# The last image's output stage two blocks at a time, its synthesis row by row behind it, in the buffers and banks of the scans

## The chip, the cores and the metric

The kernel runs on one core of a Trainium2 chip. A core has five engines that run their own instruction streams: TensorE (PE, matmuls into PSUM banks), VectorE (DVE), ScalarE (ACT), GpSimd (POOL) and SyncE (SP, used here to issue DMAs). [...] An engine takes its instructions in order, so a DMA issue that has to wait holds up every DMA issue behind it on the same engine. The metric is the device time of one launch in microseconds; lower is better.

## What is computed

The input is x, 8 images of 96 channels with 128 x 128 pixels, all float32. Two layers follow each other. The first is a row by row convolutional LSTM with a residual. The second normalises, splits each image by a wavelet transform into a low band and three high bands of 64 x 64, weights the high bands by a small attention, runs the low band through a selective scan in four directions, and puts the bands together again. Cut to what the change touches, the end of the second layer for one image is:

```
y = out_y[:, 0] + inv_y[:, 0] + wh_y + invwh_y          # sum over the four scan directions
y = layernorm(y, out_norm_w, out_norm_b) * silu(z)
x_ll = y @ out_proj_w.T                                 # "output": 192 -> 96 channels, 64 x 64
x_rec_in = concatenate([x_ll, x_high * attn])           # 4 bands for each channel
x = x + conv_transpose(x_rec_in, rec_w, stride 2)       # "synthesis": 96 channels, 128 x 128
```

## The kernel before

The kernel works through the images one after another. The scans of an image are laid out by hand as a list of slots (the loop over `s` near the end of `forward_kernel`); in each slot the engines do one scan step, and what room is left is filled with jobs of other stages. A job is a Python generator (class `Job`). Each `yield` names an engine, a cost that the planner assumes, a number of slots to wait, and the resources it takes and gives (`free`, line 481: counters of banks and buffers). `add` puts a job on the list, `write` emits as many pieces as fit and whose earlier jobs (`after`) are done, and `pin` fixes the order in which the pieces were emitted as the order of each engine. While image b is scanned, the output and synthesis of image b-1 and the wavelet analysis of image b+1 run as such jobs.

The last image has no scans of another image beside it. When its scans are over, the last lines (1209 to 1212) call `output(B - 1, ...)` and `drain(synthesis(B - 1, ...))`. `drain` sets no limits of room: it emits round after round, in the order of the job list, until all is done. There the order of the work follows from three things only: the `after` lists, the counters in `free`, and the order in which jobs were added.

`output(b, ...)` has 8 jobs, `block(j)` for 512 pixels (8 rows of the low band) each. A job loads the row-order and the column-order sums (y_d), the scan input u and the gate z from DRAM for channels 0 to 127 (first half) and 128 to 191 (second half), lines 843 to 846; adds them on POOL (849) and DVE (851); centres them with two matmuls for each half (`pf`, 859), squares on ACT (862), multiplies by the gate on DVE (864); sums the squares by matmul (`pv`, 868), takes the inverse root on ACT (871, 872); projects to 96 channels (`po`, 876, and `pq`, 883), combines on DVE (879, 886); and stores to ll_d (888). It holds six of the twelve "short" buffers. The tiles `t` and `u` serve both halves, so the second half's loads wait for the first half's adds. Each job has the job before it in `after`.

`synthesis(b, ...)` has 24 jobs, `block(g, j)`: 16 output channels (g, 6 groups) by a quarter of the image (j, 4 rows of blocks). A job loads the high bands (hi_d, 795) and the low band (ll_d, 797) into `ph`, at the upper and lower edge also a row of zeros (`zrow`, 787 and 789), and the pixels to be added to into `raw` (800). Six matmuls follow (`pd`, 811; each appears as two records in the profile), two adds on DVE (817) and four stores (820). `weights(g)` loads a group's weights (774) and scales them by the attention on ACT (777). The buffers `ph`, `raw` and `wg` have two copies each; block j of all groups depends on `after`, which for every image holds all 8 output jobs.

The scans use buffers of their own: `bt` and `ct` (five copies each, 128 x 1024), `xb` (six copies, 128 x 1024), and PSUM tiles `da` (two copies, two banks each) in the pool `psh`. The other stages' matmuls share three banks (tag "mm", counted by "bank").

Of the kernel before, what the change touches and what calls it, by code (L numbers as in the profile page):

```python
# [7 lines left out]
F32 = mybir.dt.float32  # L8
# [6 lines left out]
B, C, H, W = 8, 96, 128, 128  # L15
H2, W2 = H // 2, W // 2
L = H2 * W2
# [7 lines left out]
CH = 512  # L25
NCHK = L // CH
GN = 2
NSHORT = 12
# [28 lines left out]
def forward_kernel(ctx: ExitStack, tc: tile.TileContext, i, out):  # L57
# [29 lines left out]
    with ExitStack() as s:  # L87
# [15 lines left out]
        def place(lanes, chunk, src):  # L103
            for m in range(3):
                nc.sync.dma_start(wq[lanes, chunk, m, 0:96], src[:, m, :])
                nc.sync.dma_start(wq[lanes, chunk, m, 96:128], src[:, 3, 32 * m:32 * m + 32])
# [23 lines left out]
        for k in range(NBLK):  # L130
            xb = blk.tile([128, B, RB * W], F32, name="xb")
# [22 lines left out]
        ps = s.enter_context(tc.tile_pool(name="l0ps", bufs=2, space=PSUM))  # L154
        for k in range(NBLK):
            rows = slice(k * RB, (k + 1) * RB)
            xb = blk.tile([128, B, RB * W], F32, name="xb")
# [43 lines left out]
            for r in range(RB):  # L201
                at = [((r + 2) % 4, k + (r + 2) // 4)]
# [28 lines left out]
    with ExitStack() as s:  # L231
# [105 lines left out]
        io = s.enter_context(tc.tile_pool(name="bio", bufs=2))  # L337
        bcp = s.enter_context(tc.tile_pool(name="bbc", bufs=6))
        sp = s.enter_context(tc.tile_pool(name="bs", bufs=2))
        psh = s.enter_context(tc.tile_pool(name="bpsh", bufs=2, space=PSUM))  # L340
        psy = s.enter_context(tc.tile_pool(name="bpsy", bufs=1, space=PSUM))
        ps = s.enter_context(tc.tile_pool(name="bps", bufs=3, space=PSUM))
# [32 lines left out]
        for k in range(4):  # L375
            r, p, h0 = dtrow[k], k // 2, k % 2
# [76 lines left out]
        def pin():  # L453
            traced = tc.nc.cur_bb.bb.instructions
            for ins in traced[seen[0]:]:
                prev = pinned.get(ins.engine)
                if prev is not None:
                    tc.add_manual_dep(ins, prev.name, mybir.DependencyInfo(
                        mybir.DependencyClass.NoSync, mybir.DependencyReason.DATA), reason="order of the slots")
                pinned[ins.engine] = ins  # L460
            seen[0] = len(traced)
# [16 lines left out]
                    for r in self.give:  # L478
                        free[r] += 1

        free = dict(bank=3, short=NSHORT, raw=2, ph=2, wa=2, yf=2, dl=5)
        jobs = []
        now, at_slot = [0], [-1]

# [38 lines left out]
        def add(due, gen, after=(), take=(), give=(), urgent=0, slot=-1):  # L523
            job = Job(due, gen, after, take, give, urgent, slot)
            jobs.append(job)
            jobs.sort(key=lambda j: j.rank)
            return job

        EARLY, LATE = ("SP", "PE", "ACT"), ("DVE", "POOL")
        BANK, SHORT, NONE = ("bank",), ("short",), ()  # L530

        def hasten(job):
            if not job.done and job.rank > -1e9:
                job.due, job.rank = min(job.due, now[0]), -1e9
                for a in job.after:
                    hasten(a)

        def drain(until):

            for job in until:  # L540
                hasten(job)
            jobs.sort(key=lambda j: j.rank)
            while not all(j.done for j in until):
                big = dict(SP=1e9, PE=1e9, ACT=1e9, DVE=1e9, POOL=1e9)
                write(dict(big), EARLY)
                write(dict(big), LATE)
                now[0] += 1
                pin()
# [216 lines left out]
            return ends, put(due(NJ), attention(), after=last_bands)  # L765


        def synthesis(b, begin, end, after):
            wgs = {}

            def weights(g):
                yield "SP", 0, 0, NONE, NONE
                wgs[g] = io.tile([128, 6, 128], F32, name="wg")
                nc.sync.dma_start(wgs[g].rearrange("p t c -> p (t c)"), wr_d[:, 6 * 128 * g:6 * 128 * g + 6 * 128])
                for t in range(0, 6, 3):
                    yield "ACT", 0.61, (4 if t == 0 else 0), NONE, NONE
                    nc.scalar.activation(wgs[g][:, t:t + 3], wgs[g][:, t:t + 3], AF.Copy, scale=attn[:, g, b:b + 1])

            def block(g, j):
                cs = slice(16 * g, 16 * g + 16)  # L780
                yield "SP", 0, 0, NONE, NONE

                ph = (io.tile([128, 9, W2 + 2], F32, name="ph").rearrange("p r w -> p (r w)")
                      [:, 0:9 * W2].rearrange("p (r w) -> p r w", w=W2))
                llv = ll_d[b][cs].rearrange("c (m two w) -> c m two w", two=2, w=W2)
                if j == 0:
                    nc.sync.dma_start(ph[:, 0, :], zrow)  # L787
                if j == H2 // 16 - 1:
                    nc.sync.dma_start(ph[:, 8, :], zrow)
                for oy in range(2):  # L790

                    m0, m1 = max(8 * j - 1 + oy, 0), min(8 * j + 8 + oy, H2 // 2)
                    t = m0 - (8 * j - 1 + oy)
                    p = 64 * oy
                    nc.sync.dma_start(ph[p:p + 48, t:t + m1 - m0].rearrange("p r w -> p (r w)"),  # L795
                                      hi_d[b][g, 48 - 48 * oy:96 - 48 * oy, m0 * W2:m1 * W2])
                    nc.sync.dma_start(ph[p + 48:p + 64, t:t + m1 - m0], llv[:, m0:m1, 1 - oy, :])  # L797
                xr = io.tile([128, 9, W], F32, name="raw")[0:64, 0:8]
                for k in range(2):
                    nc.sync.dma_start(xr[32 * k:32 * k + 32], x1_d[b, g, 2 - 2 * k:4 - 2 * k, :, 8 * j + k:8 * j + k + 8, :]  # L800
                                      .rearrange("q c t w -> (q c) t w"))

                pd = None
                for k, ty in enumerate((0, 1)):
                    for tx in (1, 0, 2):
                        first = k == 0 and tx == 1
                        yield "PE", 0.87, (3 if first else 0), (BANK if first else NONE), NONE
                        if first:
                            pd = ps.tile([128, 8, W2], F32, name="pd", tag="mm")
                        c0, c1 = max(1 - tx, 0), min(W2 + 1 - tx, W2)  # L810
                        nc.tensor.matmul(pd[:, :, c0:c1], wgs[g][:, 3 * ty + tx, :],  # L811
                                         ph[:, ty:ty + 8, c0 + tx - 1:c1 + tx - 1],
                                         start=(k == 0 and tx == 1), stop=(k == 1 and tx == 2))
                for px in range(2):
                    yield "DVE", 0.68, (1 if px == 0 else 0), NONE, (BANK + ("ph",) if px else NONE)
                    v = xr[:, :, px::2]
                    nc.vector.tensor_add(v, v, pd[64 * px:64 * px + 64])  # L817
                yield "SP", 0, 2, NONE, NONE
                for q in range(4):
                    nc.sync.dma_start(out[b][cs, 32 * j + q:32 * j + 32:4, :], xr[16 * q:16 * q + 16])  # L820

            nb = H2 // 16
            done, wt = [], {}
            for g in range(GW):
                at = lambda j: begin + (end - begin) * (nb * g + j) / (nb * GW)
                wt[g] = add(at(-2), weights(g), after=[*after, *(done[-2 * nb:-nb] if g > 1 else [])])
                for j in range(nb):
                    done.append(add(at(j), block(g, j), after=[*after, wt[g]], take=("raw", "ph"), give=("raw",)))
            return done


        def output(b, begin, end, after):

            def block(j):
                o = slice(512 * j, 512 * j + 512)
# [53 lines left out]

            done = []  # L890
            for j in range(L // 512):
                done.append(add(begin + (end - begin) * j / (L // 512), block(j), after=[*after, *done[-1:]], urgent=300,
                                take=SHORT * 6, give=SHORT * 6))
            return done

# [226 lines left out]
        analysed = {0: (ends, att)}  # L1122
# [17 lines left out]
        for s in range(total):  # L1140
            at_slot[0] = s
            ci, r, q, kb, n0 = place(s)
            b, p, c = chunks[ci]
# [15 lines left out]
            if slot == 0:  # L1159
                if step == 0:  # L1160


                    if b > 0:
                        outs = output(b - 1, now[0] + 4, now[0] + 0.25 * IMAGE, turns)
# [6 lines left out]
                if ci + 1 < len(chunks):  # L1171
                    after = analysed[b + 1][0] if step + 1 == len(order) else []
# [4 lines left out]
                if p == 1:  # L1177
                    back[ci] = [add(now[0] + 2 * (8 + PASS * t), forward_sum(ci, b, c, t), after=[stored[b, c, t]],
                                    take=("yf",), urgent=1000)
# [7 lines left out]
            xb = xbs.pop(s)  # L1187
# [6 lines left out]
            if by_pool(s - 1):  # L1194
                sp1, xb = made
# [13 lines left out]
        add_up(total - 1)  # L1209
        evacuate(total - 1)  # L1210
        outs = output(B - 1, now[0], now[0], turns)
        drain(synthesis(B - 1, now[0], now[0], [*outs, analysed[B - 1][1]]))


# [62 lines left out]
```

## Time and profile before

| | us |
|---|---|
| median of 3 runs | 15879.47 (15873.98 to 15884.72) |
| time of the profiled execution | 15881.9 |
| span of the profiled execution | 15880.1 |
| end of the last scan product (DVE) | 15380.3 |
| first matmul of the last image's output | 15398.5 |
| last step of that output (DVE) | 15628.7 |
| first matmul of its synthesis | 15637.8 |
| last add of its synthesis | 15875.8 |

The busy shares over the whole span are PE 76%, DVE 74%, POOL 71%, ACT 55%. They are averages over very different stages: the first layer up to about 3000 us, then the analysis of image 0, then the scans of the eight images up to about 15383 us, then the end of the last image. Only that end is touched by the change. In rows of busy time by stretches the columns are the stretch, its length, the busy time of PE, its weight loads, DVE, ACT and POOL with the number of instructions, the granted TensorE clock (1.00 is full), the busy share of the DMA engines and the bytes per time they moved. In a timeline a row has the start, the duration, the engine ("SPq" is a DMA issue on SP), the line of the kernel, what it writes and reads, and in brackets how long the engine had been idle and what it was waiting for. A form such as 64*96 at a matmul gives the rows and columns of the array that it uses.

### The profile page before, as it was taken

How to read it: one execution, taken by the hardware profiler on the slowest of the kernel's cores; microseconds unless marked ns; L12 is line 12 of the kernel's file. 1: busy time of each engine (PE TensorE's matmuls, PEld its weight loads, DVE VectorE, ACT ScalarE, POOL GpSimd, SP SyncE). 2: the span in 40 equal slices, each digit the busy share in tenths (PEclk: the TensorE clock that was granted, in tenths of full speed). 3: DMA queues.
4: the chain of work that ended last, by engine and by line, in shares of the span. 5: the costliest groups of instructions: out<-in, count | busy, mean ns of one | idle time of the engine just before them, and what ended most of it. 6: DMA issues, size and time to landing. Idle time of an engine off the chain costs nothing. (4 is left out here: it accounts for less than half of the span.)

```text
span 15880.1 us, 146749 instructions
## 1 busy us (share of the span) xinstructions
PE 12017.8 (76%) x42850; PEld 6570.4 (41%) x42850; DVE 11728.4 (74%) x8612; ACT 8726.4 (55%) x15473; POOL 11270.4 (71%) x9544
## 2 busy tenths in 40 slices
PE   2999999586776777777777777777777777766666
PEld 0444444234444444444444444444444444444432
DVE  4333333209999988998899889888998898899871
ACT  0444444236766665666566656655665566555440
POOL 1333333009899987997798889878987898799760
PEclk9999999788887988888888888888888898877876
DMA  7333333246767777776777777777777777766653
GB/s 166 72 73 72 71 64 66 55 93 167 166 145 164 173 162 157 172 178 153 158 176 170 156 166 174 167 159 164 176 167 156 165 175 164 154 148 145 143 113 78
DMA packets 2458101, 2239.33 MB, mean 141 GB/s; under 512 B 1322929, under 2 KB 1523058, under 8 KB 2457043
## 3 DMA queue, kind: packets, MB, share of 16 engines
q1 hardware_dynamic: 1313491, 2007.56, 54.7%
q10 hardware_dynamic: 1143808, 222.38, 8.5%
q8 instruction: 344, 5.64, 0.2%
q14 instruction: 458, 3.75, 0.1%
HBM read 1862.20 MB, written 367.03 MB: 140 GB/s over the span
## 5 line engine op out<-in xcount | busy, mean ns | idle before, releaser
L1001 POOL TENSOR_TENSOR xb<-du,bt 128x1024 f32<-128x1024 f32 x3072 | 7245.7, 2362 | 330.9 <-DMA bt<-bc_d 169.6
L1025 DVE TENSOR_TENSOR_SCAN da<-da,xb 128x1024 f32<-128x1024 f32 x2304 | 5262.9, 2284 | 377.2 <-ACT da L1012 356.7
L1012 ACT ACTIVATE da<-dl,av 128x512 f32<-128x512 f32 x6144 | 4249.6, 692 | 1044.7 <-DVE hc L1191 494.7
L1039 PE MATMUL py<-ident,hc 128*128 128x128 f32 x18432 | 2882.3, 308 | 2400.6 <-DVE hc L1191 2272.9
L1039 PEld LDWEIGHTS py<-ident,hc 128*128 128x128 f32 x18432 | 2402.5, 159 | 3526.6 <-issue 1478.3
L1191 DVE TENSOR_TENSOR hc<-da,ct 128x1024 f32<-128x1024 f32 x2304 | 2813.2, 1221 | 552.5 <-DMA ct<-bc_d 390.9
L181 PE MATMUL pg<-hx,wq 128*128 128x512 f32 x4608 | 2019.7, 592 | 0.0
L1199 POOL TENSOR_TENSOR xb<-xb,ct 128x1024 f32<-128x1024 f32 x768 | 1809.3, 2356 | 99.3 <-DVE xb L1025 45.6
L1152 ACT COPY carry<-da 128x2 f32<-128x2 f32 x2016 | 319.9, 159 | 2721.8 <-DVE hc L1191 2492.7
L1025 DVE TENSOR_TENSOR_SCAN xb<-da,xb 128x1024 f32<-128x1024 f32 x768 | 1750.1, 2279 | 60.9 <-ACT da L1012 48.3
L584 PE MATMUL pd<-ph,wa 128*128 128x512 f32 x2304 | 1223.2, 663 | 262.7 <-ACT ph L578 142.3
L811 PE MATMUL pd<-ph,wg 128*128 128x504 f32 (+1 forms) x2304 | 1214.1, 659 | 204.5 <-DMA ph<-ll_d 124.4
L181 PEld LDWEIGHTS pg<-hx,wq 128*128 128x128 f32 x4608 | 871.7, 189 | 1106.7 <-issue 1106.3
L198 POOL TENSOR_TENSOR x1b<-xb,hx 96x512 f32<-96x512 f32 x256 | 302.7, 1183 | 1369.7 <-DVE hx L197 1124.4
L186 ACT ACTIVATE gate<-pg,gbias 32x512 f32<-32x512 f32 x768 | 523.3, 681 | 1185.2 <-PE pg L181 1185.2
L644 PE MATMUL pc<-xp,wc 97*128 97x512 f32 x2304 | 1143.6, 627 | 3.4 <-ACT bcs L674 3.4
L1039 PE MATMUL py<-ident,xb 128*128 128x128 f32 x6144 | 1006.5, 318 | 142.4 <-POOL xb L1199 140.5
L1039 PEld LDWEIGHTS py<-ident,xb 128*128 128x128 f32 x6144 | 879.2, 167 | 543.2 <-issue 266.7
L192 DVE TENSOR_TENSOR gate<-gate,gate 96x512 f32<-96x512 f32 x256 | 186.7, 729 | 840.9 <-ACT gate L186 840.9
L584 PEld LDWEIGHTS pd<-ph,wa 128*128 128x128 f32 x2304 | 452.7, 212 | 745.2 <-issue 439.9
L811 PEld LDWEIGHTS pd<-ph,wg 128*128 128x128 f32 x2304 | 461.7, 215 | 677.5 <-issue 580.3
L178 PE MATMUL pg<-x,wq 128*128 128x512 f32 x1536 | 703.4, 594 | 14.7 <-POOL x L168 14.7
(179 smaller groups left out, 12317.9 us busy)
## 6 DMA issues: line engine op xcount, KB each, us to landing
bt<-bc_d SPq DMA_DIRECT2D x2048, 256.0 KB
ct<-bc_d SPq DMA_DIRECT2D x2048, 256.0 KB
raw<-x_d SPq DMA_DIRECT2D x384, 288.0 KB
xb<-in_x SPq DMA_DIRECT2D x64, 1536.0 KB
du<-u_d SPq DMA_DIRECT2D x768, 128.0 KB
wa<-wa_d SPq DMA_DIRECT2D x192, 384.0 KB
xs<-in_x SPq DMA_DIRECT2D x64, 1024.0 KB
x_d<-x1b SPq DMA_DIRECT2D x792, 64.0 KB
```

The costliest lines, as they stand in the source:

```text
L178: nc.tensor.matmul(pg[m], wq[:, 3, m, :], xk[:, r, bs, 0:W], start=True, stop=False)
L181: nc.tensor.matmul(pg[m], wq[:, tap, m, :], hk[:, r, bs, tap:tap + W], start=False, stop=(tap == 2))
L186: nc.scalar.activation(gg[32 * m:32 * m + 32], pg[m][96:128], AF.Tanh, bias=gbias[96:128, m:m + 1])
L584: nc.tensor.matmul(pd, wa[:, 3 * ty + tx, :], ph[:, ty:ty + 8, tx:tx + W2], start=(ty == tx == 0), stop=(ty == 1 and tx == 2))
L644: nc.tensor.matmul(pc, wc[:, tap, d0:d0 + 128], xp[:, r + ty:r + ty + 8, tx:tx + W2], start=(tap == 0), stop=(tap == 8))
L811: nc.tensor.matmul(pd[:, :, c0:c1], wgs[g][:, 3 * ty + tx, :], ph[:, ty:ty + 8, c0 + tx - 1:c1 + tx - 1], start=(k == 0 and tx == 1), stop ...
L1001: nc.gpsimd.tensor_mul(xb, du.unsqueeze(1).to_broadcast([128, GN, CH]), bcts[k, 0])
L1012: nc.scalar.activation(das[s][:, j], inputs[ci, q][0], AF.Exp, scale=av[:, p, q, n0 + j:n0 + j + 1])
L1025: nc.vector.tensor_tensor_scan(h, da, xb, 0.0, ALU.mult, ALU.add)
L1039: nc.tensor.matmul(pys[key][:, 128 * t:128 * t + 128], hc[:, j, 128 * t:128 * t + 128], ident, is_transpose=True, skip_group_check=True, s ...
L1191: nc.vector.tensor_mul(hc, das[s], bcts[kb, 1])
L1199: nc.gpsimd.tensor_mul(xb, xb, bcts[pk, 1])
```

## The change

For the last image alone (`last`):

- `output`: a block no longer waits for the block before it but for the one two before, so two blocks can be under way. They hold all twelve short buffers.
- `synthesis` gets the output jobs as `rows`; block (g, j) waits for output blocks 2j-1 to 2j+2 (those whose rows it reads), not for all of them.
- its tiles come from the scans: `ph` from `bt` (five), `raw` from `xb` (six), weights from `ct` (five). New counters allow five blocks to hold `raw` (`scan_raw`) and four `ph` (`scan_ph`); a group's weights wait for the group five before instead of two before.
- blocks with odd j take their bank from the first half of a `da` tile (`wide`, two), those with even j from the three "mm" banks as before.

The arithmetic is the same, instruction for instruction; the number of matmuls, adds and transfers does not change.

```diff
-        free = dict(bank=3, short=NSHORT, raw=2, ph=2, wa=2, yf=2, dl=5)
+        free = dict(scan_raw=5, scan_ph=4, wide=2, bank=3, short=NSHORT, raw=2, ph=2, wa=2, yf=2, dl=5)
...
-        def synthesis(b, begin, end, after):
-            wgs = {}
+        def synthesis(b, begin, end, after, rows=None):
+
+            wgs, last = {}, rows is not None
+
+            def io_tile(shape, name, other):
+                if not last:
+                    return io.tile(shape, F32, name=name)
+                n = shape[1] * shape[2]
+                t = sp.tile([128, GN, CH], F32, name="xb", bufs=6) if other == "xb" else \
+                    bcp.tile([128, GN, CH], F32, name=other, bufs=5)
+                return t.rearrange("p j l -> p (j l)")[:, 0:n].rearrange("p (r w) -> p r w", w=shape[2])
...
-                wgs[g] = io.tile([128, 6, 128], F32, name="wg")
+                wgs[g] = io_tile([128, 6, 128], "wg", "ct")
...
-                ph = (io.tile([128, 9, W2 + 2], F32, name="ph").rearrange("p r w -> p (r w)")
+                ph = (io_tile([128, 9, W2 + 2], "ph", "bt").rearrange("p r w -> p (r w)")
...
-                xr = io.tile([128, 9, W], F32, name="raw")[0:64, 0:8]
+                xr = io_tile([128, 9 if not last else 8, W], "raw", "xb")[0:64, 0:8]
...
-                pd = None
+                pd, bank = None, ("wide",) if last and j % 2 else BANK
...
-                        yield "PE", 0.87, (3 if first else 0), (BANK if first else NONE), NONE
+                        yield "PE", 0.87, (3 if first else 0), (bank if first else NONE), NONE
                         if first:
-                            pd = ps.tile([128, 8, W2], F32, name="pd", tag="mm")
+                            pd = ps.tile([128, 8, W2], F32, name="pd", tag="mm") if bank == BANK else \
+                                psh.tile([128, GN, CH], F32, name="da")[:, 0].rearrange("p (r w) -> p r w", w=W2)
...
-                    yield "DVE", 0.68, (1 if px == 0 else 0), NONE, (BANK + ("ph",) if px else NONE)
+                    yield "DVE", 0.68, (1 if px == 0 else 0), NONE, (bank + held[1:] if px else NONE)
...
+            held = ("scan_raw", "scan_ph") if last else ("raw", "ph")
             for g in range(GW):
                 at = lambda j: begin + (end - begin) * (nb * g + j) / (nb * GW)
-                wt[g] = add(at(-2), weights(g), after=[*after, *(done[-2 * nb:-nb] if g > 1 else [])])
+                wt[g] = add(at(-2), weights(g), after=[*after, *(done[-5 * nb:-4 * nb] if last else done[-2 * nb:-nb] if g > 1 else [])])
                 for j in range(nb):
-                    done.append(add(at(j), block(g, j), after=[*after, wt[g]], take=("raw", "ph"), give=("raw",)))
+                    done.append(add(at(j), block(g, j), after=[*after, wt[g], *(rows[max(2 * j - 1, 0):2 * j + 3] if last else [])],
+                                    take=held, give=held[:1]))
...
         def output(b, begin, end, after):
+            last = b == B - 1
...
-                done.append(add(begin + (end - begin) * j / (L // 512), block(j), after=[*after, *done[-1:]], urgent=300,
+                done.append(add(begin + (end - begin) * j / (L // 512), block(j), after=[*after, *(done[-2:-1] if last else done[-1:])], urgent=300,
                                 take=SHORT * 6, give=SHORT * 6))
...
         outs = output(B - 1, now[0], now[0], turns)
-        drain(synthesis(B - 1, now[0], now[0], [*outs, analysed[B - 1][1]]))
+        drain(synthesis(B - 1, now[0], now[0], [analysed[B - 1][1]], outs))
```

In the changed program as it was built, the instructions of the end stand in this order on TensorE: output blocks 0 and 1 side by side, blocks 2 and 3, five synthesis blocks (j=0), output blocks 4 and 5, five synthesis blocks (j=1), output blocks 6 and 7, and the other 14 synthesis blocks.

## The prediction

> **What bounds the kernel now.** I read the page first (its slices show PE at 6, 6, 6, 3 tenths at the end while DVE falls to 1 and POOL to 0), then the chain of waits, then busy time by stretches. The scans end at about 15383 us. What follows is the last image's output stage and its synthesis, 497 us in which no engine is full:
>
> ```profile
> core 0: us, PE busy (x) PEld busy (x) DVE busy (x) ACT busy (x) POOL busy (x), PEclk, DMA share, GB/s
> 15383.00:15629.00 246.00, 156.90 (x160) 31.41 (x160) 33.92 (x48) 21.48 (x34) 20.12 (x16) 0.50 0.23 60
> 15629.00:15880.00 251.00, 154.64 (x288) 65.22 (x288) 32.91 (x48) 6.61 (x12) 0.00 (x0) 0.75 0.39 90
> ```
>
> The first row is 8 output blocks one after another, with the TensorE clock at 0.50 throughout; the second 24 synthesis blocks, two at a time, at 0.75. The timeline of the turn from one output block to the next:
>
> ```profile
> 15420.16 0.69 DVE L886 TENSOR_TENSOR ysum<-pq,ysum 96x512 f32<-96x512 f32 x1 [3.16 <-PE pq L883]
> 15420.92 0.34 SPq L888 DMA_DIRECT2D ll_d<-ysum  x1
> 15421.30 0.43 SPq L843 DMA_DIRECT2D ysum<-y_d  x1
> ...
> 15427.92 2.04 PE L859 MATMUL pf<-ysum,ceny 128*128 128x512 f32 x2 [7.80 <-DVE ysum L851]
> ...
> 15431.90 5.86 PE L859 MATMUL pf<-ysum,ceny 64*128 64x512 f32 x6 [1.93 <-DVE ysum L851]
> ```
>
> PE stands 7.8 us for store, loads, POOL and DVE, then 1.9 us more for the second half of the block. A block takes 29.34 us (15420.16 to 15449.50), of which 20 matmul records (two per matmul) at 0.975 us each are 19.5. The chain shows the same for a pair of synthesis blocks:
>
> ```profile
> 15816.41 0.38 SPq L795
> ...
> 15817.78 2.24 DMA ph<-ll_d
> 15820.02 0.14 issue
> 15820.16 13.20 PE pd L811 x24
> 15833.39 0.68 DVE raw L817
> ```
>
> About 20.5 us a pair: some 13 of matmul, 7 to 8 in which both buffers wait for adds, stores and new loads. The weight loads show the clock inside it: records start 0.84 us apart for about 7 of them and 0.42 after.
>
> **What moves.** Up to the end of the scans the order of instructions is the same on all five engines, so only these 497 us can change. In the changed order PE does output pair 1 (blocks 0 and 1), pair 2, five synthesis blocks (j=0 of five groups), pair 3, five blocks (j=1), pair 4, and the last 14. Loads of five synthesis blocks stand on SP between the two halves of pair 3's loads (and of pair 4's); their 20 stores stand ahead of that pair's two ll_d stores.
>
> **Start.** Five weight loads now stand ahead of the first y_d load on SP; the last waits for the last ct product (ends 15380.3), while the t load waits until 15393.0 for turn_y's landing anyway: nothing. On ACT ten scalings (0.605 us each, 6.1) come between the turn_y and turn_r stores. In the trace turn_r's issue lasts from 15385.6 to 15390.5 behind turn_y's packets; it would now start at 15391.7. Only the second-half t load needs it, and that one waits for POOL until 15397.7. Between -1.5 (turn_y has the engines alone) and +2 us; I take 0. First matmul: 15398.5, as before.
>
> **Pairs 1 and 2.** Four records of A's first and second half, then B's, run in one stream; ACT and DVE (0.6 to 0.75 us each) fit under the other block's 3.9 us. The three banks suffice: the fourth group of records needs the first's, free 1.6 us after it. Only A's two waits stay. Its second half came at 15402.6; B's loads now stand between: 15403.0. Then 38 records x 0.975 = 37.05 and the add 0.8: 15440.85. Pair 2: 0.45 store, 10.6 from first load to second half (15421.30 to 15431.90), plus 1.3 for B's 1.05 MB in between at the 290 to 390 GB/s that one-microsecond stretches show, 37.05 and 0.8: 15491.05.
>
> [...]
>
> ```profile
> 15404.00:15405.00 1.00, 1.00 (x2) 0.29 (x2) 0.00 (x0) 0.28 (x1) 0.00 (x0) 0.50 0.00 0
> ...
> 15418.00:15419.00 1.00, 1.00 (x2) 0.39 (x2) 0.00 (x0) 0.00 (x0) 0.00 (x0) 0.50 0.00 0
> ```
>
> PE is full for 17 us at half clock, in all eight blocks alike. Half of these records use 64 rows (forms 64*128, 64*96). Synthesis, with 128 rows in every record, gets the full clock after 5 us. Weighting PE's busy time by rows over 3.4 us, the output stage stays under 0.79, and the few stretches below 0.79 that raised the clock elsewhere hold 96- and 97-row records. [...] I take the row: pairing doesn't change the mix of records.
>
> **Buffers and banks.** Five ph, six raw and five weight tiles come from the scans' pools, two more banks from the da tiles (odd j). All have been idle since the scans end except the last ct, counted above; no copy or pass is added, so this costs nothing by itself, and what it gives is in the depth of five below.
>
> **Synthesis j=0 and pair 3.** PE stops at 15490.2 and goes cold. SP issues pair 3's eight first-half loads (3.6 us; 2.1 MB on the way until about +8), then the zero-row load, whose landing the next load awaits, then the rest: first matmul 12 us after the add, 15503. Five blocks are 60 records: 7 at 0.84 and 53 at 0.425 = 28.4, to 15531.4; loads (3.5 us a block on SP) keep ahead. Pair 3 follows at once. Its second-half u load waits on SP for a DVE step queued behind three blocks' adds, and its last DVE step stands behind the fifth block's adds: a hole of 1.35 us (adds 1.4, step 0.75, minus the first records). Does the clock stay full? In earlier images' outputs among the scans it does (clock 1.00 from 8412 to 8416 us with 64*96 records), and of several hundred stretches with a row share over 0.54 at full clock none dropped it; the hole makes one stretch of about 0.5. At full clock records start 0.487 apart: 40 are 19.5. With hole and add 21.65: 15553.1. At half clock it would be 19 more.
>
> **Synthesis j=1 and pair 4.** No zero rows: first matmul after 10 us, 28.4, 21.65: 15613.2. In both places SP stands at the pair's ll_d store for some 20 us with nothing behind it issued; this is the price of one queue, and it is in the 10 to 12 us.
>
> **The last 14.** Nothing overlaps but themselves. First matmul +4.5; five blocks 8.0 + 4 x 5.1 = 28.4 to +32.9. On SP: loads 2.8 us a block, 5.0 with a last-row zero load (15819.24 to 15824.26), stores 1.75. After five blocks' loads (+18.9) it stands at the stores of blocks 1 to 4, the fourth ready at +29.3, so block 6 loads at +31.1 and starts at +37.3: a hole of 4.4, clock lost. Nine more: 8.0 + 8 x 5.1 = 48.8, to +86.1, SP just ahead. Adds 1.5, then 4.3 for stores as at the end now: +91.9, **15705**. The span was 15880.1, the profiled time 15881.9, the median 15879.5; so also 15705 for the median, 175 us (1.1%) less.
>
> **Rivals.**
> 1. Likeliest, 62%: the sum, 15690 to 15725 by the unknown start, landings and hole.
> 2. Clock lost in one or both holes ahead of pairs 3 and 4: +18 or +37, 15723 to 15742, 14%. For it: windows at a share under 0.5 dropped often. Against: synthesis records, full, stand right ahead.
> 3. Landings later than taken, PE goes cold between blocks. If all five-block batches ran at 0.84 a record, j=0 and j=1 cost 22 each, the last 14 some 64: 15813; half of that, 15760, is nearer, since the present loads land in 2 us. 13%.
> [...]
> 5. Pairing does nothing since a bank or buffer serialises it: the output part keeps 235 us, synthesis gains only by five buffers: about 15800. Three banks with two in use per block speak against. 3%.
> 6. Slower. Place: the load batches. If many loads in flight land together, at the mean rate of the present synthesis (90 GB/s), five blocks' 2.8 MB take 31 us instead of some 7, before each of five batches (+125), and 3.1 MB for each of pairs 1 and 2 take 35 instead of 11 (+50): 15880, and above before once the rate is under 90 GB/s. Against: 290 to 390 GB/s where loads queue already. 4%.
>
> A measurement of this kernel tells about 0.2% (32 us) from no change. Cases 1 to 5 are all beyond it: faster 0.95; case 6 splits into same 0.02 and slower 0.03. The range takes in case 4 and reaches through case 2 into half of case 3: 15670 to 15765.
>
> **What would show it.** Right: output pairs 49 to 51 us apart at clock 0.50 before the first synthesis block; clock 1.00 through pairs 3 and 4, each about 20 us; PE holes of 10 to 12 us ahead of both five-block runs and one of 4 us within the last 14. Wrong: clock 1.00 in pair 1 (rule, not row), 0.50 in pair 3, PE idle between single synthesis blocks, or a first matmul later than 15400.

## The result, and the profile after

| | before | after |
|---|---|---|
| median of 4 runs, us | 15882.09 (15873.98 to 15885.77) | 15733.85 (15721.82 to 15759.49) |
| ratio | | 0.9912, 95% interval 0.9899 to 0.9924 |
| span of the profiled execution | 15880.1 | 15735.5 |
| end of the last scan product (DVE) | 15380.3 | 15368.5 |
| from there to the end of the span ("the tail" below) | 499.8 | 367.0 |

The kernel became 148 us faster (0.9%). The forecast was 175 faster, 15705 us; 15734 lies within its range. The scans are the same stream of instructions in both kernels, yet their end moves by some 12 us between these two profiles (and by up to 47 between the runs below). So the tail is the quantity to compare: it lost 132.8 us, where the forecast's sum has 15705.1 - 15380.3 = 324.8 left, a loss of 175.

The first view of the changed kernel is the busy time by stretches of the tail, cut where the granted TensorE clock changes (columns as in the rows shown of before):

```profile
core 0: us, PE busy (x) PEld busy (x) DVE busy (x) ACT busy (x) POOL busy (x), PEclk, DMA share, GB/s
15373.00:15503.00 130.00, 82.75 (x86) 17.68 (x87) 16.98 (x24) 15.37 (x27) 12.59 (x10) 0.50 0.36 85
15503.00:15530.00 27.00, 25.72 (x61) 11.18 (x60) 9.51 (x14) 0.18 (x1) 2.72 (x2) 1.00 0.57 136
15530.00:15581.00 51.00, 37.40 (x40) 7.88 (x39) 5.50 (x8) 4.82 (x8) 2.52 (x2) 0.50 0.32 84
15581.00:15608.00 27.00, 25.72 (x61) 11.27 (x59) 10.51 (x14) 0.00 (x0) 2.92 (x2) 0.99 0.64 132
15608.00:15653.00 45.00, 39.66 (x43) 8.51 (x42) 5.57 (x9) 5.00 (x8) 0.00 (x0) 0.51 0.15 35
15653.00:15735.00 82.00, 71.67 (x164) 31.30 (x162) 19.20 (x28) 1.12 (x2) 0.00 (x0) 0.98 0.59 135
```

Row 1 is output pairs 1 and 2, cold as forecast. Rows 2 and 4 are the two runs of five synthesis blocks, at full clock. Rows 3 and 5 are pairs 3 and 4 with the idle time behind them, and they are cold: the forecast had them at 1.00. The timeline of TensorE shows where it happens:

```profile
15387.00 2.07 PE L872 MATMUL pf<-ysum,ceny 128*128 128x512 f32 x2 [15.99 <-DVE ysum L864]
15395.88 13.66 PE L872 MATMUL pf<-ysum,ceny 64*128 64x512 f32 x14 [6.81 <-DVE ysum L864]
...
15498.52 27.95 PE L821 MATMUL pd<-bt,ct 128*128 128x512 f32 x60 [13.80 <-DMA bt<-ll_d]
15526.31 1.02 PE L872 MATMUL pf<-ysum,ceny 128*128 128x512 f32 x2
15528.61 12.10 PE L872 MATMUL pf<-ysum,ceny 64*128 64x512 f32 x14 [1.28 <-DVE ysum L864]
15540.64 2.02 PE L881 MATMUL pv<-t,on 128*96 128x512 f32 x2
...
15577.72 27.61 PE L821 MATMUL da<-bt,ct 128*128 128x512 f32 x60 [13.61 <-DMA bt<-ll_d]
```

Sixty synthesis records run without a gap in 28 us (before: 24 records in 13.2, then 7 to 8 idle). Behind them the first two records of pair 3 still take 0.5 us each; then comes a hole of 1.28 us (forecast 1.35), and from there a pair of records takes 2.02 us, twice as long: the clock fell at 15530.3, 1.7 us after the hole. The hole is as small as forecast, and behind it the clock is 0.50.

The chain of waits of the changed kernel gives the start of the tail:

```profile
15373.24 8.37 DMA y_d<-turn_y
15381.62 3.20 DMA t<-y_d
15384.89 1.27 POOL ysum L862
15386.18 7.47 DMA t<-y_d
15393.79 1.26 POOL ysum L862
```

The load of the second half of block A (`t`, issued 15386.18) takes 7.47 us against 3.20 for the first half; block B's 1.05 MB were issued ahead of it.

### The profile page after: what moved, and what is told of

It is laid out like the page before. It is cut to its first block, busy times and chain, and to the rows that moved or that the text cites. A ratio compares the mean times of both kernels' runs of the same rounds, so it can differ in the third digit from the quotient of the medians.

```text
span 15735.5 us, 146695 instructions
## 1 busy us (share of the span) xinstructions
PE 11996.4 (76%) x42850; PEld 6581.3 (42%) x42850; DVE 11727.1 (75%) x8612; ACT 8726.1 (55%) x15473; POOL 11272.9 (72%) x9544
## 5 line engine op out<-in xcount | busy, mean ns | idle before, releaser
L821 PE MATMUL pd<-ph,wg 128*128 128x504 f32 (+1 forms) x2016 | 1063.0, 654 | 123.1 <-DMA ph<-ll_d 38.2
L1017 POOL TENSOR_TENSOR xb<-xb,ac 128x2 f32<-128x2 f32 x2688 | 545.9, 203 | 210.8
```

Of the source, the lines that this page charges most:

```text
L1017: nc.gpsimd.tensor_add(xb[:, :, e0], xb[:, :, e0], ac[:, n0:n0 + GN])
```

## The experiments

All of them start from the changed kernel; none leaves out a part of the computation.

### The hole and the clock

**Filling the hole.** Two matmuls that nothing reads stand in the hole of pairs 3 and 4.

```diff
                     for k_i, (_, k) in enumerate(parts):
                         nc.tensor.matmul(pf, ...)
+                        if last and j in (4, 6) and part_i == k_i == 0:
+                            idle = psy.tile([128, CH], F32, name="py")
+                            for _t in range(2):
+                                nc.tensor.matmul(idle, ident, ys[0], start=True, stop=True)
```

> In the profile of the changed kernel pairs 3 and 4 lose the full clock about 4 us after they begin, and take 38.6 and 38.9 us from first matmul to last add instead of the 21.65 predicted. This kernel adds two matmuls (four records of 128 rows, about 1.7 us at full clock) on an idle bank between A's first and second records of pairs 3 and 4, so that the hole of 1.28 us is filled; the output is the same. Theory hole (the idle 1.28 us takes the row share of one 3.4 us stretch under 0.5): clock 1.00 through both pairs, each about 21 to 22 us, tail from the last scan product to the end 33 to 35 us shorter than 367.0. Rival mix (records of which half use 64 rows cannot hold the full clock, hole or no hole): clock 0.50 after two stretches, pairs still 37 to 39 us, tail within 4 us of 367.

Measured: 15734.07 us (ratio 0.9893, 0.9878 to 0.9909); tail 335.2, so 31.8 less than the changed kernel's. The scans of this profile happened to end 33 us later (15401.2), which hides it in the median; the ratio, against the kernel before measured beside it, shows it (0.9893 against 0.9912). TensorE in pair 3:

```profile
15558.15 1.02 PE L872 MATMUL pf<-ysum,ceny 128*128 128x512 f32 x2
15559.01 1.88 PE L877 MATMUL py<-ysum,ident 128*128 128x512 f32 x4
15560.82 7.23 PE L872 MATMUL pf<-ysum,ceny 64*128 64x512 f32 x14
15567.98 1.10 PE L885 MATMUL pv<-t,on 128*96 128x512 f32 x2
```

With the filler (x4) in place of the idle 1.28 us, the same 14 records take 7.23 us instead of 12.10. From its first to its last record pair 3 takes 22.2 us instead of 37.8. So in this run the 64-row records did not lower the full clock; with the hole ahead of them, in the changed kernel, it fell to 0.50.

**All records with 128 rows.** The second half of a block loads channels 64 to 191 instead of 128 to 191, with zero weights for the 64 channels that are doubled. The number of records is the same.

```diff
+                halves2 = ((0, 128), (64, 128)) if last else parts
-                for part_i, (d0, m) in enumerate(parts):
+                for part_i, (d0, m) in enumerate(halves2):
...
+        full = sp.tile([128, CH], F32, name="du", bufs=5)
+        nc.vector.memset(full, 0.0)
+        nc.vector.memset(full[64:128, 192:288], 1.0 / DI)
+        nc.sync.dma_start(full[64:128, 0:192], ceny[0:64, 1, :])
...
```

> All matmuls of the last image's output use 128 rows: the second half loads channels 64 to 191 and has zero weights for the doubled ones, so the output is the same; its loads are twice as large. Row theory (the clock follows PE's busy time weighted by rows): pairs 1 and 2 reach the full clock some 5 us after their stream begins and take about 15 us less each, pairs 3 and 4 keep the clock over the hole (row share of the stretch 0.6 or more) and take about 20 us less each; tail 65 to 75 us shorter than 367.0, time about 15665. [...]

Measured: 15701.77 us (0.9868, 0.9852 to 0.9884), tail 299.2. TensorE in pair 1, second half of block A onward:

```profile
15434.42 2.08 PE L875 MATMUL pf<-ysum,du 128*128 128x512 f32 x2 [5.69 <-DVE ysum L867]
15436.28 1.91 PE L875 MATMUL pf<-ysum,ceny 128*128 128x512 f32 x2
15437.99 1.85 PE L875 MATMUL pf<-ysum,du 128*128 128x512 f32 x2
15439.68 1.02 PE L875 MATMUL pf<-ysum,ceny 128*128 128x512 f32 x2
15440.54 1.02 PE L875 MATMUL pf<-ysum,du 128*128 128x512 f32 x2
...
15530.72 1.13 PE L875 MATMUL pf<-ysum,du 128*128 128x512 f32 x2 [1.28 <-DVE ysum L867]
15531.68 1.02 PE L875 MATMUL pf<-ysum,ceny 128*128 128x512 f32 x2
```

After 5.3 us of records with 128 rows the clock rises: a pair of records goes from 2.08 to 1.02 us, and the 38 records take 19.2 us instead of 37.1. In pairs 3 and 4 the hole of 1.28 us is still there, and the clock stays at 1.00 across it (the last two lines). In the changed kernel pair 1 ran its 37.1 us without a gap at 0.50.

The edit also widened four of a block's 20 records from 64 to 128 columns, so by itself it doesn't tell rows from columns. The whole profile of the changed kernel does. In its trace the granted clock is 0.50 or 1.00, and every time at one level is a multiple of 3.41 us long (in the tail 51.20 from 15530.32 and 27.31 from 15581.51), but for the last, which the span cuts off. Cut into stretches of 3.41 us and weighted by the rows in use, the busy share of TensorE sorts those of this profile: of the stretches at half clock, none of 546 under 0.75 was followed by full clock, and 416 of 417 over 0.84 were (82 of the 142 between). Of those at full clock none of 2781 over 0.52 was followed by half clock, and all 436 under 0.40 were. Weighted by rows times columns, stretches that raised the clock and stretches that did not mix from 0.48 to 0.84, and 82 of 411 at half clock without any gap stayed there. So in this profile the change of clock goes with the share weighted by rows, better than with the share weighted by rows and columns; between 0.75 and 0.84, and between 0.40 and 0.52, the rows leave it open.

**The same kernel again.** Is the loss certain, or a matter of where the hole falls against the 3.41 us stretches?

> The changed kernel itself once more. The stretch that holds the hole in pairs 3 and 4 had a row share of 0.47 in the first profile and the clock fell; in the kernel with single output blocks stretches of 0.47 to 0.49 with the same hole kept it. Theory edge (the share lies at the limit, and where the hole falls in the free-running stretches decides): tail 367, 350 or 333 us by how many of the two holes lose the clock, with the start of the output's first matmul and the synthesis runs the same within 2 us. If the drop were a fixed property of pairing, the tail is 367 within 3 us again.

Measured: 15760.08 us (0.9919, 0.9904 to 0.9934), tail 368.3, clock lost in both holes again. By itself that spoke against the edge theory. But three later runs hold the same tail, instruction for instruction, and differ only in the setup before the images. Two (tails 366.6 and 365.7) lost the clock in both holes, and one (337.7) kept it in both. Weighting TensorE's time in the stretch that holds the hole by the rows in use gives a share of 0.47 in all eight lost cases of this tail, and 0.48 and 0.49 in the two kept ones. In the lost cases the hole starts 0.06 to 0.84 us after the edge of a stretch and lies wholly within it; in the kept ones it starts 0.10 us before an edge and 1.23 us after one. So in this tail the place of the hole against the edges goes with the outcome. That is not all of it: in the run with single blocks (below) two holes with 0.47 kept the clock, one of them 0.10 us behind an edge, and in the run with stores on ACT two stretches with 0.46. What decides near 0.47 stays open.

### Which part of the change gives what

**Pairs without rows behind them.** Synthesis waits for the whole output again.

```diff
-        drain(synthesis(B - 1, now[0], now[0], [analysed[B - 1][1]], outs))
+        drain(synthesis(B - 1, now[0], now[0], [*outs, analysed[B - 1][1]]))
```

> The output two blocks at a time as in the changed kernel, but all of it before the synthesis, which keeps the five buffers and two more banks. By the sum of the prediction with measured terms: four pairs at 46.6 and 3 x 51.8 us are 202 us instead of 230 in the kernel before; synthesis of 24 blocks with five buffers about 4.6 + 24 x 5.1 and a few holes of 2 to 4 us with cold restarts, 145 to 155 instead of 251: tail 375 to 385 us. So if the row-by-row order is what saves most, this is much longer than 367 (over 400); if depth of buffers and pairing do, it is within 20 us of 367.

Measured: 15878.67 us (0.9988, 0.9981 to 0.9995), tail 470.7. The edit went further than the expectation says: without `rows` the synthesis is no longer `last`, so it lost the five scan buffers and the wide banks too and ran two blocks at a time as before. The run therefore prices the pairing alone: 499.8 - 470.7 = 29 us, four pairs of about 52 us for eight blocks of 29.34.

**Rows behind single blocks.** Synthesis as in the change, output one block at a time.

```diff
-after=[*after, *(done[-2:-1] if last else done[-1:])]
+after=[*after, *done[-1:]]
```

> The synthesis row by row behind the output with the scans' buffers as in the changed kernel, but the output one block at a time. Three single blocks, then three times five synthesis blocks with an output block behind each and one before the next, then nine synthesis blocks: 3 x 29.3 + 3 x (10 + 28) + 3 x 21 + 2 x 29.3 + 66 = about 390 us from the first matmul instead of 348.5, tail about 408. If pairing is worth what the prediction gave it (8 us a pair in the stream and a hole of 10 to 12 us less), this is 35 to 45 us longer than the changed kernel; if pairing does nothing, the same.

Measured: 15788.66 us (0.9927, 0.9911 to 0.9943), tail 380.5, less than the 408 worked out for it. The sum had every output block cold; but the block right behind each run of five synthesis blocks kept the clock (18 records in 9.3 us, the others 17.6), which is 8 us three times. So the rows and the buffers are the larger part: 499.8 - 380.5 = 119 us. Pairing on top of them is worth only 13.5 with the clock lost, and 43 where it is kept (tail 337.7).

### The idle time ahead of the synthesis, and within its last run

**Loads first.** In pairs 3 and 4 the output's loads are planned one round later, so that the synthesis loads stand ahead of them on SP.

```diff
                 t, u = None, None
+                if last and j > 3:
+                    yield "SP", 0, 0, NONE, NONE
+                    yield "SP", 0, 1, NONE, NONE
```

> Pairs 3 and 4 start one planning round later, so that four of the five synthesis blocks' loads stand ahead of the pair's first-half loads on SP instead of behind them. If the pair's 2.1 MB in front and the waits for their landing make the 13.8 and 13.6 us holes ahead of the synthesis runs, these shrink to 5 to 7 us each and the tail by 14 to 17 us against the same kernel without it (351, or 317 to 334 where the clock holds). If the wait is that for the ll_d store or the zero row, they stay over 10 us.

Measured: 15764.85 us (0.9915, 0.99 to 0.9929), tail 342.5. The idle time of TensorE ahead of the two runs fell from 13.8 and 13.6 us to 6.4 and 5.3. In return the hole in pair 3 grew, as the timeline of this run shows:

```profile
15554.83 6.66 SPq L830 DMA_DIRECT2D out<-xb  x12
...
15562.14 0.55 SPq L860 DMA_DIRECT2D t<-y_d  x1
...
15567.23 1.22 PE L875 MATMUL pf<-ysum,ceny 64*128 64x512 f32 x1 [5.45 <-DVE ysum L867]
```

Twelve stores of synthesis results (6.66 us of issues) now stand ahead of the second half's `t` load, TensorE waits 5.45 us, and pair 3 runs cold (37.1 us). In pair 4 the hole stayed at 1.33 and the clock held (19.6). The gain in the lead is real (15.7 us); on one queue part of it comes back as a hole. Of the 24.5 us by which the tail is shorter than the changed kernel's, 16.2 are pair 4's kept clock; the order of loads, less what it costs elsewhere, nets about 8.

**Stores on ACT.** The last image's 96 synthesis stores are issued by ACT.

```diff
-                yield "SP", 0, 2, NONE, NONE
+                yield ("ACT" if last else "SP"), 0, 2, NONE, NONE
-                    nc.sync.dma_start(out[b][...], ...)
+                    (nc.scalar if last else nc.sync).dma_start(out[b][...], ...)
```

> The last image's synthesis stores are issued by ACT instead of SP. If SP standing at stores of earlier blocks makes the two holes of 3.5 and 1.6 us among the last 14 blocks (and the restart at half clock after the first), these go, and the 14 blocks take 75 to 77 us from first to last matmul instead of 81.1; the holes ahead of the synthesis runs stay 12 to 14 us. If they come from the loads' landing or from buffers, no change there.

Measured: 15751.64 us (0.9906, 0.9892 to 0.9921), tail 359.2. A miss: the last 14 blocks take 83.6 us from the first matmul to the last, 81.1 in the changed kernel. The hole of 3.5 us after five blocks is gone (eight blocks run in 47.8 us), but three holes of 1.0 to 1.6 come behind the eighth, tenth and twelfth. ACT also issues stores between the output's steps, and pair 3 gets two holes of 2.1 and 1.0 us; it kept the clock all the same (23.8 us instead of 37.8), which is more than the 7.8 us by which the tail is shorter. The waits of SP in the last 14 blocks (total in us, number, longest) show what still held the loads back:

```profile
SPq L806 <- DMA out<-xb: 12.6, 5, 5.0
SPq L804 <- DMA out<-xb: 11.9, 3, 5.0
```

Loads into `bt` wait 24.5 us for stores out of `xb`, another buffer, issued on another engine. In the trace the DMAs of both engines share eight completion semaphores (in the changed kernel's, 9727 issues of SP and 1216 of ACT stand on the same eight), and the load at 15720.95 takes the semaphore of the store that ACT issued at 15718.99. So with ACT as a second engine for the stores, SP's loads still waited 24.5 us for them.

**All three**, with the weights for 128 rows put together ahead of the images and kept in DRAM:

> All three: 128 rows in all output records (weights prepared at the start of the layer and fetched in one load), synthesis loads first, stores on ACT. From the tail of 299.2 us with 128 rows alone: 5 us less at the start (one load instead of three and two fills after the scans), 14 to 17 less ahead of the synthesis runs, 6 less in the last 14: 270 to 276. If the parts share a cause (all wait for DMA landing), 285 or more.

Measured: 15565.17 us (0.9793, 0.9776 to 0.9809). The expectation missed twice. The tail is 306.1, worse than with 128 rows alone (299.2): TensorE idles 8.4 and 6.0 us within the two synthesis runs ahead of pairs 3 and 4, which are without a gap in the changed kernel. And the scans, which none of the three edits touches, end at 15238.5, 130 us or more earlier than in any run before. Of the edits only the setup stands ahead of the scans, and four runs went into it.

### Why the scans became shorter

The setup took one short buffer, cleared it, filled it by three DMAs and stored it by a fourth into a new DRAM tile of 256 KB. The order of all other instructions is the same on every engine.

```diff
+        full_d = dram.tile([128, CH], F32, name="full_d")
+        full = short("full")
+        nc.vector.memset(full, 0.0)
...
+        nc.sync.dma_start(full_d, full)
```

**The short buffer alone** (`short("full")` and one memset):

> The changed kernel with one thing more: ahead of the second layer's images one short buffer is taken and cleared, and nothing reads it. All later short tiles so lie one buffer further on; order of instructions on all engines and all DMAs as in the changed kernel. It asks where the 150 us shorter scans of the run with three edits come from. Theory T (the turn of the short buffers): scans end near 15240, time near 15605 (tail 366). Theory D (the four DMAs and the DRAM tile of that setup): scans end between 15369 and 15409 as in the changed kernel, time 15735 to 15775. Theory N (neither: the runs differ by chance or by the weight tile at the end): as D here.

Measured: 15762.93 us (0.9914, 0.9899 to 0.9929); scans end at 15415.8, tail 366.6. Not the buffer.

**Four DMAs and a DRAM tile of 128 KB:**

> The changed kernel with one thing more: ahead of the second layer's images SP issues four DMAs of 49 KB each into a new DRAM tile of 128 KB that nothing reads. The later DRAM tiles so lie 128 KB further on and the later DMAs take the completion semaphore four places on; order of instructions otherwise as in the changed kernel, no short buffer is taken. Theory D: scans end near 15240, time near 15605. Theory T: scans end 15369 to 15409, time 15735 to 15775. Theory N: as T here.

Measured: 15715.83 us (0.9881, 0.9867 to 0.9896); scans end at 15353.2, tail 365.7. The end is 15 us earlier than in the changed kernel's profile, but 63 earlier than in the run with the short buffer alone, which ran on the same chip; with equal tails (365.7 and 366.6) the medians are 47 apart, and the four times of each do not overlap (15700 to 15721, 15748 to 15784). So these DMAs or the 128 KB by which they move the later buffers do shorten the scans, though not by the 130 that were sought.

**128 rows with the setup**, nothing else:

> The output records with 128 rows, their weights put together ahead of the images (setup with one short buffer, four DMAs, a DRAM tile of 256 KB) and loaded in one DMA at the end; loads and stores of the synthesis in the changed kernel's order and on SP. The tail was 299.2 with three small DMAs and two fills after the scans (first matmul 23.5 after the scans' end instead of 18.5): now 294 to 299. If the setup alone shortens the scans (theory T or D), they end near 15240 and the time is 15535 to 15545, below the 15565 of the run with three edits; if it took the loads first or the stores on ACT as well, the scans end at 15370 to 15410 and the time is about 15680.

Measured: 15552.12 us (0.978, 0.9763 to 0.9796), the fastest of all; scans end at 15264.4, tail 289.9. So the setup shortens the scans, and neither the order of loads nor the stores on ACT are needed; with them the tail is 16 us longer (306.1).

**The same four DMAs, the DRAM tile 256 KB:**

```diff
-        full_d = dram.tile([64, CH], F32, name="full_d")
+        full_d = dram.tile([128, CH], F32, name="full_d")
         for _t in range(4):
-            nc.sync.dma_start(full_d[:, 0:192], ceny[0:64, 1, :])
+            nc.sync.dma_start(full_d[0:64, 0:192], ceny[0:64, 1, :])
```

> The run with four extra DMAs again, with one number changed: their DRAM tile has 256 KB instead of 128 KB (the same four DMAs into its first rows, the same semaphores, no short buffer taken). In the program as built, the DRAM buffers of images 0 to 6 (hi_d to y_d) so lie 256 KB further on than in the changed kernel, as in the two runs with short scans (15238.5 and 15264.4), against 128 KB in the run with four DMAs (15353.2) and none in the others (15369 to 15416); those of image 7 stay where they were. Theory A (the addresses): scans end between 15235 and 15270, time 15600 to 15640 (tail 366), with 1471 to 1482 us for each of images 2 to 6 instead of 1498 to 1506, and no gain in image 7. Theory C (it takes the short buffer, the fills and the four DMAs together, not the place of the buffers): scans end 15340 to 15410, time 15705 to 15775.

Measured: 15612.98 us (0.9815, 0.9798 to 0.9833); scans end at 15283.2. Between this run and the one with 128 KB only the place of the buffers in DRAM differs, and the scans are 70 us shorter. They end 13 us later than theory A allowed, and images 2 to 6 in the table take up to 6 us more than it said, so the place explains most of the gain, not all. The time from the start of one image's scans to the next, in us, with the images counted from 0:

| image | changed kernel | +128 KB | +256 KB | 128 rows (+256 KB) |
|---|---|---|---|---|
| 1 | 1492.1 | 1489.2 | 1478.8 | 1474.8 |
| 2 | 1498.3 | 1501.6 | 1487.7 | 1481.4 |
| 3 | 1505.3 | 1498.7 | 1484.8 | 1481.1 |
| 4 | 1501.9 | 1501.9 | 1485.6 | 1482.3 |
| 5 | 1501.8 | 1494.9 | 1477.3 | 1480.5 |
| 6 | 1505.7 | 1488.6 | 1474.5 | 1471.5 |
| 7 (to the end of the scans) | 1428.7 | 1436.0 | 1440.2 | 1438.9 |

In the program as built the buffers of image 7 are the only ones that did not move, and it gains nothing. But image 0, not in the table, moved too and became longer: 1368.2 us with 128 KB, 1377.5 with 256. What image 3 gains is read from the groups of VectorE: the last part of a row is its idle time before these instructions and what ended it. First the changed kernel, then the one with the 256 KB tile:

```profile
L1038 DVE TENSOR_TENSOR_SCAN da<-da,xb 128x1024 f32<-128x1024 f32 x288 | 658.0, 2285 | 54.2 <-ACT da L1025 46.5 <-POOL xb L1014 6.4 <-POOL xb L1017 1.0
L1204 DVE TENSOR_TENSOR hc<-da,ct 128x1024 f32<-128x1024 f32 x288 | 351.7, 1221 | 75.5 <-DMA ct<-bc_d 57.4
```

```profile
L1042 DVE TENSOR_TENSOR_SCAN da<-da,xb 128x1024 f32<-128x1024 f32 x288 | 658.0, 2285 | 49.6 <-ACT da L1029 47.7 <-POOL xb L1018 1.5
L1208 DVE TENSOR_TENSOR hc<-da,ct 128x1024 f32<-128x1024 f32 x289 | 352.8, 1221 | 51.6 <-DMA ct<-bc_d 32.9
```

The instructions take the same time. What shrank is the wait for the landing of `ct`, from 57.4 to 32.9 us, 24.5 of it, and the image became 20.5 us shorter. Over images 1 to 6 VectorE's idle time ahead of these products is 462 us with the short buffer alone, 403 with 128 KB, 326 with 256 KB and 328 with 128 rows and the setup. Why those loads land sooner from the other place was not traced further.

TensorE in pair 3 of this run also shows the kept clock over the unchanged hole:

```profile
15443.17 1.02 PE L876 MATMUL pf<-ysum,ceny 128*128 128x512 f32 x2
15445.47 7.23 PE L876 MATMUL pf<-ysum,ceny 64*128 64x512 f32 x14 [1.28 <-DVE ysum L868]
```

## Why the prediction was right, and where its sum was off

The direction, the mechanism and the range held. Each term against the profile of the changed kernel, in us:

| term of the sum | forecast | measured | difference |
|---|---|---|---|
| start to the first output matmul | 18.2 | 18.5 | +0.3 |
| pair 1, to its last add | 42.35 | 46.7 | +4.3 |
| pair 2 | 50.2 | 51.8 | +1.6 |
| lead of the first synthesis run | 12 | 13.1 | +1.1 |
| five synthesis blocks | 28.4 | 27.8 | -0.6 |
| pair 3 | 21.65 | 38.5 | +16.9 |
| lead of the second run | 10 | 12.9 | +2.9 |
| five synthesis blocks | 28.4 | 27.4 | -1.0 |
| pair 4 | 21.65 | 38.9 | +17.2 |
| last 14 blocks | 91.9 | 91.5 | -0.4 |
| sum | 324.8 | 367.0 | +42.2 |

- **The term that was mis-sized** is pairs 3 and 4, "At full clock records start 0.487 apart: 40 are 19.5". The records started 0.975 apart behind the hole. The text had this as its second case (18 or 37 more, 15723 to 15742, 14%), and that is what happened: 34.1 more. The step that failed is the judgement against it, "synthesis records, full, stand right ahead". They do, but the stretch behind which the clock fell is the one with the hole. The text itself put that at "about 0.5" and knew that none over 0.54 dropped; at 0.47 it did. The profile of before could have priced this: of its stretches at full clock with a share of 0.50 to 0.54, 3 of 97 were followed by half clock, of those with 0.46 to 0.48, 10 of 30. The run with the hole filled and the run with the 256 KB tile show the forecast's value: 22.2 and 21.9 us from a pair's first record to its last, against 37.8.
- **Luck in the total.** The scans end 11.8 us earlier in the profile of the changed kernel than in that of before, and by the medians some 15 of the 148 us are not the tail's. With the scans' end of before, the measured tail gives 15380.3 + 367.0 = 15747: within the range, but above the second case's interval, in which the median lies.
- **Rows and the clock.** The sum has pairs 1 and 2 at 0.50, as the output stage of before showed, and they ran 37.1 us each without a gap at 0.50. With 128 rows in every record they rose to 1.00 after 5.3 us and took 19.2. The reason given, the rows in use, agrees with the padding and with the count of stretches. The range goes down to 15670 for a case with the full clock in these pairs; no run shows that case for them as they are, and the runs showed 0.50 in its place.
- **Pairs 1 and 2** were forecast at 0.50 and "49 to 51 us apart"; their first matmuls are 54.1 apart (15387.00 to 15441.07). The 4.3 us of pair 1 are the load of A's second half: it came 8.9 us after the first matmul, not 4.5, behind B's megabyte. In one-microsecond stretches the loads moved 254 to 367 GB/s up to 15389, and from there to 15395 only 135 to 195, where the text took 290 to 390 throughout; why the rate fell was not traced.
- **The leads** were 12 and 10; TensorE's idle time was 13.8 and 13.6. The reason given, a load that awaits the landing of the zero row, is in the profile for the first. The last line is from the waits of SP:

```profile
15489.73 0.44 SPq L796 DMA_DIRECT2D bt<-zrow  x1
15490.57 0.32 SPq L804 DMA_DIRECT2D bt<-hi_d  x1
15491.25 0.33 SPq L806 DMA_DIRECT2D bt<-ll_d  x1
15495.73 0.30 SPq L804 DMA_DIRECT2D bt<-hi_d  x1
...
SPq L804 <- DMA bt<-zrow: 8.0, 5, 4.1
```

  From the end of the third issue (15491.58) to 15495.73 SP issues nothing. The second run has no zero row and idles as long, so the missing zero row was not worth the 2 us that the sum took off. There SP's waits name older loads (of `t`, `u`, `z` and the sums), 4.4 us together, which are the shared eight semaphores again: in the trace the nine issues from 15569.25 to 15576.49 each start 0.02 us after the landing of the eighth DMA before, which has the same semaphore.
- **The last 14** came as forecast, 91.5 for 91.9, with a hole of 3.5 for 4.4 and another of 1.6 that the sum had as "SP just ahead".
- **The rivals.** No sign of loads slow enough for the slower case: the three stretches of synthesis in the first view moved 132 to 136 GB/s, not 90, and both five-block runs are without a gap. Nothing serialised the pairs: two blocks take about 52 us, one alone 29.34.

## What to carry to other kernels

Where a stretch runs cold, look at the rows that its records use: here 37.1 us without a gap stayed at 0.50 while half of the records used 64 rows, and padding them to 128, with no record more, brought a pair's matmuls to 19.2 us. In pairs 3 and 4 a hole of 1.28 us cost some 16 us, and filling it or widening the rows brought them back; so price such a hole by a run rather than at its length. And where the end of a kernel is improved, compare the end alone: here the scans ahead of it ended up to 47 us apart with the same instructions, and 70 us apart with nothing changed but the place of their buffers.

## What the runs showed of the hardware that was not expected

- The scans' time changed with the place of the images' buffers in DRAM. A tile of 256 KB instead of 128 KB, of which nothing more is used, moved the end of the scans from 15353 to 15283 us. Without any move (neither tile) it lay between 15369 and 15416 in nine profiles, of the changed kernel and of edits of it. The two 256 KB runs that also took the short buffer ended still earlier, 15264 and 15239; the rest of that difference is open.
- In the run with stores on ACT, loads on SP waited for stores of another engine out of another buffer, with which they share eight completion semaphores: 24.5 us of SP's waits in the last 14 blocks.
- The clock was kept in some and lost in others of the same sequence of 60 full records, two more, and a hole of 1.28 us: with 64-row records behind it, lost in eight cases of ten with pairs, at some 16 us each, and in none of three with single blocks. Single runs of the changed kernel spread over 38 us (15721.82 to 15759.49); how many of them kept the clock was not seen, since only the first is profiled.
